# A planner's port rule, the RMS powers and the last norm's sums changed in a four-layer graph network kernel

## The chip, the core and the metric

The kernel runs on one core of a Trainium2 chip. The metric is the device time of one execution in microseconds (us), here the median of several. TensorE (PE) multiplies matrices, VectorE (DVE) and ScalarE (ACT) work on elements, GpSimd (POOL) takes powers, SyncE (SP) issues the transfers (DMA).

## What is computed

There are 32 independent graphs. Each has 512 nodes with 256 features (`x`) and a 512x512 weighted adjacency matrix (`adj`), and goes through four layers, all in fp32. Cut to what matters:

```python
# layer 0
x = layernorm(x + relu(((1 + eps) * x + adj @ x) @ W1 + b1) @ W2 + b2)       # 256 -> 512 -> 256
# layer 1
h = adj @ (x @ W.T + b);  x = layernorm(x + where(h > 0, h, alpha * h))
# layer 2
h = layernorm(x) * gamma + beta
x = layernorm(x + (x + relu((adj @ h) @ W_rel + b_rel + h @ W_root)))
# layer 3
h = (epsilon * x + adj @ x) @ W1 + b1                                        # 256 -> 1024
h = silu(h * rsqrt(mean(h * h, -1) + 1e-6) * rms_weight)                     # RMS norm, one factor per node
x = layernorm(x + h @ W2 + b2)
```

`layernorm` subtracts the mean over a node's features and divides by the square root of the variance plus 1e-5.

## The kernel before

**Blocks and products.** A graph's nodes lie as 128 partitions x 4 chunks (`NC = 4`). Each product (`aggregate`, `dense_feat`, `dense_add`) is cut into 2x2 blocks and made of seven block products instead of eight (`seven`, line 642): m1 to m7 are multiplied by TensorE into three PSUM banks, and between them VectorE or ScalarE reads a bank out (`take`, `put`). A bank is used by two or three products one after the other: the later product accumulates on the earlier one's result, so that it has to wait until the earlier one's `take` has read the bank. The block sums that the method needs (`left_sums`, `right_sums`, lines 660 and 668) are additions of VectorE. A graph has 106 matmuls with 256 columns and 112 with 128; the profile has two records for each.

**Order of the work.** The kernel first records every operation of all 32 graphs (`Plan.add`, line 247) with what it reads and writes, and with an estimated duration: the engine's busy time, and a tail until its result can be used (`vector_time`, `scalar_time`, `power_time` and so on, lines 32 to 63). `Plan.order` (line 350) then runs through time on these estimates. At each step it takes the engine that can start something first, and the operation of the lowest rank there. The rank is the graph's number times `period` plus the due time of the operation (`needs`, line 320). Up to five graphs are under way at once (`FLIGHT`), sharing 36 SBUF rooms and 8 banks. `best` (line 344) tries the entries of `RULES` (line 92) and takes the one whose plan ends first. The program then issues the operations in this order, each engine in its own queue; on the chip semaphores alone decide when one starts. An operation that ScalarE or VectorE can do goes to the one that the plan chose. As every operation is issued from the same line, the profile puts nearly all under L294.

**The port in the plan.** VectorE instructions with two operands in SBUF (`TWO_OPERANDS`, line 79) and GpSimd's are marked `port` (line 284). In the plan, a marked VectorE instruction holds GpSimd off until its end, and a GpSimd instruction holds marked VectorE work off for `PORT` = 0.25 us from the power's own start (lines 426 to 429).

**Norms.** Every inverse square root is a power of -0.5 by GpSimd (`inv_sqrt`, line 567): one of 128 partitions x 4 elements in each of layers 0, 2 and 3 (last norm), one of 128x8 in layer 1 (two scalings), one of 128x4 for the RMS norm. `Norm` (line 887) has ScalarE sum each chunk twice (`total`: an Identity with a sum, then a Square with the mean as bias), `NormOnVector` (line 938) has VectorE do it with bn_stats and bn_aggr. Layer 3's last norm uses `NormOnVector`, the others `Norm`.

**The RMS factor.** In layer 3 the squares of the 1024 features are added up by VectorE (`acc`). `column_sums` (line 866) reduces them with a transposing reduction and three additions to 32 partitions x 16. `everywhere` (line 975) then turns this into one factor per node along a row of all partitions: `by_token` (line 882) spreads the sums over 128 partitions x 4 in four small instructions, the power is taken, four more (`square`) bring it back to 32x16, a 32x32 transpose follows, and two transfers through DRAM (`line`) copy it to all partitions. The first and the last graph (`alone`) use TensorE for this instead.

**Transfers.** All go through SP's queue. `move` (line 304) has a `late` figure, extra time that the plan assumes: 1.0 for the loads of `x` and `adj`, 0.0 for `carry` (line 564), which moves blocks of transposed features within SBUF.

Of the kernel before, what the change touches and what calls it, by code (L numbers as in the profile page):

```python
# [20 lines left out]
def span(ap):  # L21

    n = 1
    for d in ap.shape[1:]:
        n *= d
    return n
# [33 lines left out]


def power_time(n):
    return 0.3 + n * 0.21, 0.04

# [10 lines left out]


TWO_OPERANDS = ("tensor_add", "tensor_sub", "tensor_mul", "scalar_tensor_tensor")
PORT = 0.25  # L80


SOON = 0.03
# [5 lines left out]

RULES = [(40, 2, 12, 0.25), (40, 2, 20, 0.25), (45, 2.5, 20, 0.25)]


class Pool:
# [104 lines left out]
class Op:  # L200
# [10 lines left out]
    behind: int = 0  # L211
    then: list = field(default_factory=list)
    start: float = 0.0
    way: str = ""


class Plan:
# [132 lines left out]
    def order(self, period, pace, last, near):  # L350

        final = max(op.graph for op in self.ops) - self.flight + 1
        rank = [
            (min(op.graph, final) * period + max(op.graph - final, 0) * last + need, i)
            for i, (op, need) in enumerate(zip(self.ops, self.needs(pace, near)))
        ]
        behind = [op.behind for op in self.ops]
        ready = [dict.fromkeys(op.ways, 0.0) for op in self.ops]
        left = {}
        for op in self.ops:  # L360
            left[op.graph] = left.get(op.graph, 0) + 1
            for r in op.rooms:
                r.clear()
                r.pool.clear()
        free = dict.fromkeys(("tensor", "vector", "scalar", "gpsimd", "sync"), 0.0)
        oldest, wire, lanes = 0, 0.0, [0.0] * LANES
        port = dict.fromkeys(free, 0.0)
        can_start = {i for i, n in enumerate(behind) if not n}
        done = []
        while can_start:  # L370
            while oldest in left and not left[oldest]:
                oldest += 1
            room_at = {}

            def rooms_free(op):

                first = [r for r in op.rooms if r.index is None]
                if not first:
                    return 0.0
                if op.graph - oldest >= self.flight:  # L380
                    return None
                at, taken = 0.0, {}
                for r in first:
                    pool = r.pool
                    if pool not in room_at:
                        room_at[pool] = pool.free()
                    whole, halves = room_at[pool]
                    k = taken.get((pool, False), 0)
                    if not r.whole and k < len(halves):
                        taken[pool, False] = k + 1  # L390
                        at = max(at, halves[k][0])
                        continue
                    n = taken.get((pool, True), 0)
                    taken[pool, True] = n + 1
                    n += pool.spare[min(op.graph - oldest, len(pool.spare) - 1)]
                    if n >= len(whole):
                        return None
                    at = max(at, whole[n][0])
                return at

            best = {}
            for i in can_start:
                op = self.ops[i]
                wait = rooms_free(op)
                if wait is None:
                    continue
                if op.kbytes and "sync" in op.ways:
                    wait = max(wait, lanes[0])
                at = {
                    e: max(free[e], wait, ready[i][e], port[e] if op.port else 0.0) for e in op.ways  # L410
                }
                way = min(
                    at, key=lambda e: at[e] + sum(op.ways[e][0]) + YIELD * (op.yields and e == "vector")
                )
                best.setdefault(way, []).append((at[way], rank[i], i))
            if not best:
                return 1e12, None
            t, engine = min((min(c)[0], e) for e, c in best.items())
            soon = t + (1e-6 if engine == "tensor" else SOON)
            _, t, i = min((r, s, i) for s, r, i in best[engine] if s <= soon)  # L420
            op = self.ops[i]
            op.start, op.way = t, engine
            busy, tail = op.ways[engine][0]
            free[engine] = t + busy
            end = t + busy + tail
            if op.port and engine == "vector":
                port["gpsimd"] = end
            elif op.port and engine == "gpsimd":
                port["vector"] = t + PORT
            if op.kbytes:  # L430
                wire = max(wire, t + ADVANCE) + wire_time(op.kbytes)
                end = wire + op.late + AFTER
                if engine == "sync":
                    lanes = [*lanes[1:], end]
            for r in op.rooms:
                if r.index is None:
                    r.pool.take(r)
                r.left -= 1
                r.until = max(r.until, end + 0.1)
            left[op.graph] -= 1  # L440
            for n, result in op.then:
                behind[n] -= 1
                for e in ready[n]:
                    if e != engine or e != "tensor" and result:
                        ready[n][e] = max(ready[n][e], end + HAND[e])
                if not behind[n]:
                    can_start.add(n)
            can_start.remove(i)
            done.append(op)
        return max(op.start for op in done), done  # L450
# [3 lines left out]
def tile_gnn_stack(ctx: ExitStack, tc: tile.TileContext, a: dict, out: bass.AP):  # L454
# [107 lines left out]
        plan.do(o, way)  # L562

    def carry(o, x):
        plan.move(o, x, o.shape[0] * span(o) / 256)

    def inv_sqrt(o, x):
        n, p = span(o), o.shape[0]
# [11 lines left out]
    def small(*shape):  # L580
        return Part(Room(smalls)).shaped(*shape)
# [25 lines left out]
    def constant(name, shape):  # L607
        return const.tile(shape, F32, tag=name, name=name)
# [22 lines left out]
    ctx.enter_context(nc.allow_non_contiguous_dma(reason="small vectors, once"))  # L631
    ident = constant("ident", [P, P])
    make_identity(nc, ident)
    mhalf = constant("mhalf", [P, 2 * NC])
    scraps = [constant(f"scrap{i}", [P, D]) for i in range(2)]
    nc.vector.memset(scraps[0], 0.0)
    nc.vector.memset(mhalf, -0.5)
    for tile_of_few in smalls.tiles:
        nc.vector.memset(tile_of_few, 0.0)

# [52 lines left out]
    class Adjacency:  # L693
# [3 lines left out]
        def __init__(self, b):  # L697

            self.halves = [room(HC, N) for _ in range(2)]
            for m in range(NC):  # L700
                chunk = self.halves[m // HC][:, m % HC, :]
                plan.move(chunk, a["adj"][b][:, m, :], P * N / 256, late=1.0)
            a11, a12, a21, a22 = (
                self.halves[j][:, :, i * TH : (i + 1) * TH] for i in range(2) for j in range(2)
            )
            self.left = dict(m1=a11, m2=a12, m4=a22)
            self.a21 = a21
# [174 lines left out]
    def by_token(o, sums, *ops):  # L882

        for q in range(P // Q):
            ts(o[q * Q : (q + 1) * Q], sums[:, q :: P // Q], *ops)
# [88 lines left out]

    def everywhere(sums, ops):

        few = small(2, NC)
        ve, power = few[:, 0, :], few[:, 1, :]
        by_token(ve, sums, *ops)
        inv_sqrt(power, ve)  # L980
        if alone():
            o = bank(N)
            for c in range(NC):
                flip(o[:, c * P : (c + 1) * P], power[:, c : c + 1].spread(P, P))
        else:
            few = small(2, Q)
            square, turned = few[0:Q, 0, :], few[0:Q, 1, :]
            for q in range(P // Q):
                ts(square[:, q : N // Q : P // Q], power[q * Q : (q + 1) * Q], 1.0, None, ALU.mult)
            plan.do(turned, vector("transpose", Q, square))  # L990
            o, line = short(N), next(lines)
            name = line.tensor.name
            plan.move(line.rearrange("(m i) -> m i", i=Q), turned[0 : N // Q], N / 256, into=name)
            plan.move(o, line.partition_broadcast(P), P * N / 256, late=0.8, outof=[name])
        return o
# [17 lines left out]

    def load_x(b):
        x = tok()
        plan.move(x, a["x"][b].rearrange("(p c) d -> p c d", c=NC), N * D / 256, late=1.0)
        return x

    def layer0(x, adjacency):
# [53 lines left out]
    def layer3(x, adjacency, b):  # L1073
# [17 lines left out]
        for q in range(0, FH, 2):  # L1091
# [2 lines left out]
                act(hT.chunk(f), hT.chunk(f), AF.Silu, scale=w_3[:, f : f + 1])  # L1094
            for m, t in dense_sums([hT.pair(q)], [hT.pair(FH + q)]).items():
                right[m] = right.get(m, []) + t
        norm = NormOnVector(x)
        dense_add(x, right, A2_3, norm.half)
        norm.scales((1.0, LN_EPS))
        y = norm.scaled()  # L1100
# [56 lines left out]

    with tc.manual_schedule():
        for op in plan.best():
            op.ways[op.way][1]()  # L1160


# [35 lines left out]
```

## Time and profile before

| | us |
|---|---|
| median of 3 runs | 2349.52 (2348.96 to 2350.26) |
| the profiled execution | 2349.14 |
| its span in the profile | 2347.2 |
| PE busy, DVE busy | 2305.1, 2209.5 |
| ACT busy, POOL busy | 1516.7, 233.3 |
| granted TensorE clock | 0.999 |
| VectorE waiting for TensorE, in all | 70.0 (52 times) |
| 128x4 powers, 128x8 powers, mean of one | 1.151 (128 of them), 2.671 (32) |

The profile comes from one execution. A row of a timeline says when an instruction (or several of one kind) started, how long it took, its engine, its source line, what it wrote and read (`room` is SBUF, `ps` is PSUM, `few` a small SBUF tile), its shape and, in brackets, how long the engine had idled before it and who released it. A row with "x3" runs from the first one's start to the last one's end; the end of one lies a little after the start of the next, so the cost of one in a queue is read from start to start. The chain of work that ended last is followed back from the last instruction, at each step to what released it. Busy time of PE is modelled at its ends, so a PE that is called busy can still hide short waits.

### The profile page before, as it was taken

What the parts mean: (1) busy time and instruction counts of PE and PEld (TensorE: products, weight loads), DVE (VectorE), ACT (ScalarE), POOL (GpSimd) and SP (SyncE); (2) the same over time, 40 slices, a digit from 0 to 9 for tenths busy, and PEclk for the clock granted to TensorE, in tenths of its full rate; (3) what the DMA queues carried; (4) which work ended last, traced back from release to release, by engine and by line L of the source; (5) the groups of instructions that cost most, each with busy time, mean ns of one, the idle gap of its engine ahead of it and who ended that gap; (6) DMA issues with size and microseconds to landing.
All of it is one profiled execution on the core that took longest, in us unless ns stands there. A gap on an engine that the chain in (4) does not pass through costs nothing.

```text
span 2347.2 us, 40710 instructions
## 1 busy us (share of the span) xinstructions
PE 2305.1 (98%) x14002; PEld 2095.8 (89%) x14002; DVE 2209.5 (94%) x5850; ACT 1516.7 (65%) x3918; POOL 233.3 (10%) x166
## 2 busy tenths in 40 slices
PE   9999999999999999999999999999999999999998
PEld 7888998999999999989999999999999989888897
DVE  8998999999999999999999999999999999998988
ACT  4675667666676665676666766657666567566764
POOL 0100011101011101011011111010110101011001
PEclk9999999999999999999999999999999999999999
DMA  7001222122221122211222211222112221121001
GB/s 238 21 17 19 64 55 52 30 59 61 56 58 27 56 59 64 54 37 43 60 62 54 59 25 57 61 57 57 35 48 59 63 57 48 37 59 50 19 10 45
DMA packets 223454, 122.79 MB, mean 52 GB/s; under 512 B 142864, under 2 KB 194320, under 8 KB 223248
## 3 DMA queue, kind: packets, MB, share of 16 engines
q1 hardware_dynamic: 223248, 120.20, 19.2%
q8 instruction: 110, 1.80, 0.3%
q14 instruction: 96, 0.79, 0.1%
HBM read 78.92 MB, written 24.97 MB: 44 GB/s over the span
## 4 chain that ended last, share of the span: by engine, by line
PE 84%; DVE 12%; DMA 1%; issue 1%; ACT 1%; SPq 0%; POOLq 0%; DVEq 0%; ACTq 0%
PE ps L294 84%; DVE room L294 10%; DVE few L294 2%; ACT room L294 1%; ACT scrap L294 0%; DMA diagonal<-room 0%; SPq L312 0%; DMA L_gnn_eps<-in_L_gnn_eps_dram 0%; DMA room<-in_x_dram 0%; DMA room<-room 0%; DMA room<-in_adj_dram 0%; DVE A L294 0%; POOLq L1194 0%; DVE L_gnn_W L294 0%; DVEq L294 0%
## 5 line engine op out<-in xcount | busy, mean ns | idle before, releaser
L294 PE MATMUL ps<-room,room 128*128 128x256 f32 x3584 | 931.7, 380 | 6.1 <-ACT room L294 2.6
L294 DVE TENSOR_TENSOR room<-room,room 128x512 f32<-128x512 f32 (+1 forms) x1360 | 778.0, 591 | 4.1 <-DMA room<-in_adj_dram 1.7
L294 PEld LDWEIGHTS ps<-room,room 128*128 128x128 f32 x3584 | 613.2, 191 | 62.7 <-ACT room L294 6.5
L294 DVE TENSOR_TENSOR room<-ps,room 128x256 f32<-128x256 f32 (+1 forms) x1344 | 599.1, 471 | 66.9 <-PE ps L294 65.6
L294 PE MATMUL ps<-L_gnn_W,room 128*128 128x128 f32 (+1 forms) x3584 | 583.2, 291 | 4.4 <-DVE room L294 2.2
L294 PEld LDWEIGHTS ps<-L_gnn_W,room 128*128 128x128 f32 x3584 | 539.0, 191 | 50.0 <-DVE room L294 5.0
L294 PEld LDWEIGHTS ps<-A,room 128*128 128x128 f32 x3072 | 466.3, 191 | 68.0 <-issue 17.1
L294 PE MATMUL ps<-A,room 128*128 128x128 f32 x3072 | 492.0, 276 | 17.3 <-DVE few L294 13.4
L294 POOL TENSOR_TENSOR few<-few,mhalf 128x4 f32<-128x4 f32 (+1 forms) x160 | 232.6, 1455 | 2108.2 <-DVE few L294 2084.2
L294 PE MATMUL ps<-room,L_gnn_W 128*128 128x256 f32 x1536 | 419.3, 380 | 3.1 <-DVE room L294 3.1
L294 ACT ACTIVATE room<-room,few 128x256 f32<-128x256 f32 x580 | 316.4, 597 | 121.7 <-DVE few L294 121.6
L294 ACT ACTIVATE room<-ps 128x256 f32<-128x256 f32 x514 | 187.9, 376 | 248.4 <-PE ps L294 247.1
L294 DVE TENSOR_TENSOR room<-room 128x256 f32<-128x256 f32 (+1 forms) x640 | 314.3, 496 | 34.4 <-DMA room<-room 13.4
L294 ACT ACTIVATE room<-ps,L_gnn_b_c 128x256 f32<-128x256 f32 x768 | 310.6, 478 | 50.7 <-PE ps L294 50.3
L294 PE MATMUL ps<-room,A 128*128 128x256 f32 x1152 | 323.4, 380 | 0.4 <-DVE room L294 0.2
L294 ACT ACTIVATE room<-room 128x1024 f32<-128x1024 f32 (+2 forms) x260 | 242.1, 945 | 122.4 <-DVE room L294 119.0
L294 PEld LDWEIGHTS ps<-room,L_gnn_W 128*128 128x128 f32 x1536 | 271.2, 191 | 32.2 <-DVE room L294 6.4
L294 ACT ACTIVATE scrap<-room 128x256 f32<-128x256 f32 x384 | 157.4, 411 | 172.3 <-DVE room L294 168.5
L294 ACT ACTIVATE scrap<-room,few 128x256 f32<-128x256 f32 x384 | 191.5, 499 | 77.6 <-DVE few L294 74.9
L294 PEld LDWEIGHTS ps<-room,A 128*128 128x128 f32 x1152 | 204.0, 191 | 21.5 <-ACT room L294 0.7
L294 ACT ACTIVATE room<-room,L_gnn_rms_weight_c 128x512 f32<-128x512 f32 x256 | 170.6, 711 | 28.0 <-DVE room L294 27.9
L294 DVE TENSOR_SCALAR few<-few 32x4 f32<-32x4 f32 (+2 forms) x792 | 119.0, 158 | 6.5 <-ACT scrap L294 0.6
(56 smaller groups left out, 1153.8 us busy)
## 6 DMA issues: line engine op xcount, KB each, us to landing
room<-in_adj_dram SPq DMA_DIRECT2D x128, 256.0 KB, 5.0
room<-in_x_dram SPq DMA_DIRECT2D x32, 512.0 KB, 6.0
out_dram<-room SPq DMA_DIRECT2D x32, 512.0 KB, 3.2
room<-room SPq DMA_DIRECT2D x480, 32.0 KB, 2.0
diagonal<-room SPq DMA_DIRECT2D x62, 128.0 KB, 1.8
room<-in_adj_dram SPq DMA_DIRECT2D x124, 64.0 KB, 1.9
room<-diagonal SPq DMA_DIRECT2D x62, 128.0 KB, 2.3
room<-line SPq DMA_DIRECT2D x30, 256.0 KB, 3.3
```

What stands on the lines that cost most here:

```text
L294: getattr(getattr(self.nc, engine), method)(to, *(put(x) for x in args), **kw)
```

## The change

It has five parts. `power_time`, `PORT` and `RULES` get other numbers, and the plan's port rule is another: after a VectorE instruction whose result a power uses, marked VectorE work is held off for 0.35 us from that instruction's end, and no longer by the power's start. Where the plan leaves VectorE idle for that reason, the program issues small memsets of a tile of its own (`pause`). The RMS power is taken directly on the 32 partitions x 16 of the sums, so that `by_token` and `square` go, but for the first and the last graph. Layer 3's last norm is a `Norm`, again but for these two. And the transfers are planned with longer `late` figures. The diff, its core:

```diff
 def power_time(n):
-    return 0.3 + n * 0.21, 0.04
+    return 0.3 + n * 0.18, 0.2 + 0.06 * n
...
-PORT = 0.25
+PORT = 0.35
...
-RULES = [(40, 2, 12, 0.25), (40, 2, 20, 0.25), (45, 2.5, 20, 0.25)]
+RULES = [(42, 2, 20, 0.5), (42, 2, 12, 0.25)]
...
+        powers = {i for i, op in enumerate(self.ops) if op.port and "gpsimd" in op.ways}
...
-            free[engine] = t + busy
+            free_before, free[engine] = free[engine], t + busy
             end = t + busy + tail
-            if op.port and engine == "vector":
-                port["gpsimd"] = end
-            elif op.port and engine == "gpsimd":
-                port["vector"] = t + PORT
+            if engine == "vector":
+                idle = t - max(free_before, ready[i][engine])
+                op.pause = idle if op.port and t == port[engine] else 0.0
+                if op.port:
+                    port["gpsimd"] = end
+                if any(n in powers for n, _ in op.then):
+                    port["vector"] = t + busy + PORT
...
     def carry(o, x):
-        plan.move(o, x, o.shape[0] * span(o) / 256)
+        plan.move(o, x, o.shape[0] * span(o) / 256, late=1.2)
...
-    mhalf = constant("mhalf", [P, 2 * NC])
+    mhalf = constant("mhalf", [P, N // Q])
...
-                plan.move(chunk, a["adj"][b][:, m, :], P * N / 256, late=1.0)
+                plan.move(chunk, a["adj"][b][:, m, :], P * N / 256, late=1.6)
...
     def everywhere(sums, ops):
-        few = small(2, NC)
-        ve, power = few[:, 0, :], few[:, 1, :]
-        by_token(ve, sums, *ops)
-        inv_sqrt(power, ve)
         if alone():
+            few = small(2, NC)
+            ve, power = few[:, 0, :], few[:, 1, :]
+            by_token(ve, sums, *ops)
+            inv_sqrt(power, ve)
...
         else:
-            few = small(2, Q)
-            square, turned = few[0:Q, 0, :], few[0:Q, 1, :]
-            for q in range(P // Q):
-                ts(square[:, q : N // Q : P // Q], power[q * Q : (q + 1) * Q], 1.0, None, ALU.mult)
+            few, turned = small(2, Q), small(Q)[0:Q]
+            ve, square = few[0:Q, 0, 0 : N // Q], few[0:Q, 1, :]
+            ts(ve, sums, *ops)
+            inv_sqrt(square[:, 0 : N // Q], ve)
             plan.do(turned, vector("transpose", Q, square))
...
-        plan.move(x, a["x"][b].rearrange("(p c) d -> p c d", c=NC), N * D / 256, late=1.0)
+        plan.move(x, a["x"][b].rearrange("(p c) d -> p c d", c=NC), N * D / 256, late=1.6)
...
-        norm = NormOnVector(x)
+        norm = (NormOnVector if alone() else Norm)(x)
...
         for op in plan.best():
+            if op.pause and op.way == "vector":
+                for _ in range(round(op.pause / 0.11)):
+                    nc.vector.memset(pause, 0.0)
             op.ways[op.way][1]()
```

More of the change, by code (lines that the diff above doesn't have):

```diff
@@ L213 @@
     start: float = 0.0
+    pause: float = 0.0
     way: str = ""
@@ L637, in tile_gnn_stack @@
     nc.vector.memset(mhalf, -0.5)
+    pause = constant("pause", [P, 48])
     for tile_of_few in smalls.tiles:
```

## The prediction

> **What bounds the kernel now.** I read the page's first section, then the chain of work that ended last, then the timelines of single engines around the one place where that chain leaves TensorE.
>
> ```profile
> span 2347.2 us, 40710 instructions
> ...
> PE 2305.1 (98%) x14002; PEld 2095.8 (89%) x14002; DVE 2209.5 (94%) x5850; ACT 1516.7 (65%) x3918; POOL 233.3 (10%) x166
> ...
> PE 84%; DVE 12%; DMA 1%; issue 1%; ACT 1%; SPq 0%; POOLq 0%; DVEq 0%; ACTq 0%
> ```
>
> TensorE is busy 98% of the time, so at most the rest, and what hides inside "busy", can be won. The chain in order of time, over two graphs in the middle:
>
> ```profile
> 1148.40 70.31 PE ps L294 x428
> 1218.71 0.01 issue
> 1218.72 1.17 PE ps L294 x8
> 1219.89 0.42 DVE room L294
> 1220.31 0.09 DVE few L294
> 1220.40 0.06 issue
> 1220.46 70.31 PE ps L294 x428
> ```
>
> The same piece begins at 1148.40 and at 1220.46: a period of 72.06 us, one graph, and the whole-span list of long pieces repeats it from 214 to 1872, 23 times. In each, TensorE runs 70.31 us unbroken and then waits for one VectorE instruction. How much is that worth? In the timeline of PE, 26 matmul records of 256 columns start 0.216 us apart (5.78 us less one 0.38, by 25) and 8 of 128 columns 0.111 apart. A graph has 106 matmuls of 256 and 112 of 128 columns, each two records: 212 x 0.216 + 224 x 0.1113 = 70.7 us. So a period holds 72.06 - 70.7 = 1.35 us that are not matmul work, about 1.0 at this break and the rest in tenths. For all 14002 records the same sum is 2271 us; of the other 76 us, 31 are in the 23 periods, about 10 before the first and after the last matmul, and about 35 in the start-up (to 214) and the last graphs (from 1872). The break itself, PE first and then DVE:
>
> ```profile
> 1218.11 0.60 PE L294 MATMUL ps<-room,room 128*128 128x256 f32 x2
> 1218.72 1.16 PE L294 MATMUL ps<-A,room 128*128 128x128 f32 x8
> 1220.46 1.13 PE L294 MATMUL ps<-A,room 128*128 128x128 f32 x8 [0.58 <-DVE few L294]
> ```
>
> ```profile
> 1217.59 1.08 DVE L294 TENSOR_TENSOR room<-ps,room 128x256 f32<-128x256 f32 x3
> 1218.59 0.68 DVE L294 TENSOR_TENSOR room<-room,room 128x512 f32<-128x512 f32 x1
> 1219.18 0.68 DVE L294 TENSOR_SCALAR few<-few 32x4 f32<-32x4 f32 x4
> 1219.89 0.42 DVE L294 TENSOR_TENSOR room<-ps,room 128x256 f32<-128x256 f32 x1
> ```
>
> These are layer 2's dense products (weights A, from `A_2`). Two records of 256 from 1218.11 should end their issue at 1218.54, and the next start at 1218.72; eight of 128 should give way at 1219.61, and the next start at 1220.46: 0.18 + 0.85 lost. In the built order the product that waits (m3) accumulates in the bank of m5, and m5's take is the add at 1219.89. VectorE has not idled: that take stands behind a 512-wide add and the four `square` instructions of the RMS power. So TensorE's one steady wait is VectorE being late.
>
> **The change, part by part.**
>
> *RMS powers on 32 partitions.* Out go, in 30 graphs (not the first and last, which are alone), four `by_token` and four `square` instructions; in comes one of 32x16. The row above prices four at 0.70 us (1219.18 to 1219.89), the new one at 0.15 by the 32x16 adds: 2 x 0.70 - 0.15 = 1.25 us of VectorE per graph. All four squares stood directly ahead of the awaited take, and the four `by_token` (0.67 us, at 1214.19) five microseconds ahead of it, with VectorE hardly idle between. In the built order of the changed kernel layer 2's seven products stand as before (between m5 and m3 again a product of four, one 256-column matmul and another product of four), but between the takes of m1 and m5 there are now one 512-wide add (0.60), one 128x4 (0.07) and the 32x32 transpose (0.12), 0.79 us, where there were 1.30. So the take comes 0.51 us earlier by the order alone, and up to 1.03 (the whole break) if the 0.5 us of the `by_token` carries through: I take 0.75.
>
> The power itself grows from 4 to 16 elements a partition. Its rows:
>
> ```profile
> 1150.15 1.01 POOL L294 TENSOR_TENSOR few<-few,mhalf 128x4 f32<-128x4 f32 x1 [6.03 <-DVE few L294]
> ...
> 1175.95 3.02 POOL L294 TENSOR_TENSOR few<-few,mhalf 128x8 f32<-128x8 f32 x1 [12.76 <-DVE few L294]
> ```
>
> The 128x8 power takes 1.64 in some graphs (at 169.05) and 3.02 in the periods. From 1.01 and 1.64 each element costs 0.158: 16 of them about 2.9 us, an estimate; with the delay of the 128x8 (1.38 for 8) doubled, 5.7. In the new order the work on VectorE between the instruction that releases it and the transpose that reads it sums to 6.1 us. So either way nothing waits. If VectorE ran ahead of that, the price would be the difference, some 2 us once a graph on the row's way to layer 3, whose transfers (1.3 and 3.3 us) lie ahead of products that are not due.
>
> *Two-operand work kept off the start of powers.* The plan now lets a one-operand or PSUM instruction follow each release. Where VectorE did adds of two SBUF operands through the start, the 128x8 power took 3.02; where an add from PSUM followed it (169.05), 1.64. So the powers will be short: 1.4 us for the 8, some 0.3 for the 4s. But it is worth nothing on the path: the late power's reader stands at 1179.59, after its end at 1178.97, and in the list of waits VectorE waited for GpSimd 2.9 us in the whole run, TensorE 0.3. Nothing becomes late instead. The pauses are 22 memsets in the built program, none in its repeating part; at 0.11 us (the 128x64 memset) at most 2.4 us, and I take 0.5, since they stand in the start-up and the end, half of which is VectorE's.
>
> Here a rule speaks against the longer power. The Trainium skill, "SBUF — State Buffer", "Who interferes with whom", says that VectorE with two SBUF inputs and a GpSimd instruction that reads SBUF exclude each other, the later one blocked until the first is done. By it each power would stop VectorE to its end: 2.9 us more a graph, 60 us in 21 periods, and the change would lose. The row says otherwise: within the power from 1150.15 to 1151.16 a 512-wide add of two SBUF operands starts at 1150.73 and takes 0.66 us, its usual time (mean 678 ns over 912). Only GpSimd is delayed. I go by the row: 0.
>
> *Last norm's sums by ScalarE.* Out go four BATCH_NORM_STATS2 (0.31 from start to start) and four aggregates (0.09) per graph; in come on ScalarE four Identity sums (0.42 from start to start, at 1169.27) and four Square sums (0.50, at 1174.40). VectorE gets 1.6 us, ScalarE 3.7. One scaling also moves to ScalarE in the new order (0.33 off, 0.55 on). ScalarE goes from 1084/23 = 47.1 to 51.3 us of a 72 us period: room enough in sum; that a copy is held up is the slow rival below. The functions are ones already in use, so no table loads come.
>
> *Longer transfers planned* (`late`), and new ranks: no instruction is added, and SP's queue holds the same 32 issues a graph. In a period VectorE has one wait for such a transfer (0.64 us, at 1197.16), and right after it waits 1.77 us for TensorE (at 1199.63), which hides it: I count 0, bounds -2 to 4 for the edges, where loads do end waits.
>
> **The sum.** VectorE loses 1.25 + 1.6 + 0.33 = 3.2 us of 68.6 (1578/23) a graph: 65.4 of 72, so it is no longer within 5% of TensorE's 70.7. Periods: the built order repeats exactly for 21 graphs, 21 x 0.75 = 16 us. Start-up and end: nine graphs of the thirty lie there, 9 x 3.2 = 29 us of VectorE work; the chain there is about a third VectorE, and part of the gaps are loads, so of about 35 lost us I take 6. Bounds: 12 if it follows VectorE's share in full, and -4, since the repeating part begins one graph later in the new order and a start-up graph loses some 5 us (18 to 214) where a period loses 1.35. Together 16 + 6 - 0.5 = 21.5. The profiled execution took 2349.14 (span 2347.2 and 1.9 around it); its difference from the median 2349.52 is 0.4. 2349.1 - 21.5 = 2327.6; I say **2328**.
>
> **The rivals.**
> - *The wait only moves.* VectorE's spare time falls where nobody waits, and another take is 1 us late each period in the new order, as greedy orders do. For: with VectorE at 65 of 72 there are still stretches without a gap. Against: the same seven products have lost just what held them. It leaves the edges: 2349 - 6 = 2343 (2338 to 2349).
> - *All waits go.* With VectorE clear, TensorE runs at its pitch: 21 x 1.35 = 28, edges 12: 2309 (2305 to 2317). Against: a third of the 1.35 are tenths from many takes.
> - *ScalarE becomes late (slower).* In the new order four sums (2 x 0.42 + 2 x 0.50 = 1.84 us) stand right ahead of a ScalarE copy out of an aggregate's bank. Between a product there and the next into its bank lie at least 1.1 us of other matmuls; less the copy (0.36) and about 0.3 of hand-off, 0.45 is to spare. If all 1.84 falls on it, TensorE waits 1.4 a period: 21 x 1.4 = 29, less 21.5: 2357. It decides from 0.45 + 21.5/21 = 1.5 us of delay. Against: ScalarE idles 20 us in 72, and TensorE waited 5.5 us for it in the run before.
>
> **How the numbers follow.** A measurement here tells about 0.2% (4.7 us) from no change. Chances: main case 0.58 (own range 2318 to 2338), the wait moves 0.20, all go 0.14, ScalarE 0.08. Faster by over 0.2% (below 2344.8): 0.57 + 0.14 + 0.12 = 0.83; the same: 0.10; slower: 0.07. For 8 in 10 the range takes in the likelier part of each neighbour: 2309 to 2345.
>
> **What would show it.** Right: a period near 71.3 us in the chain with its break at layer 2's products gone or below 0.3; VectorE near 2110 busy, ScalarE near 1640; 128x8 powers at 1.64, the 32x16 near 2.9 and no VectorE wait for it. Wrong: a period still near 72 with another instruction as releaser; TensorE waiting for ScalarE's copies; VectorE adds longer than 0.7 us inside the long power; or start-up and end longer than 214 and 475 us by more than the periods win.

## The result, and the profile after

| us | before | after |
|---|---|---|
| median (5 runs each, same chip) | 2350.26 (2348.96 to 2350.80) | 2339.10 (2337.50 to 2340.12) |
| profiled execution, its span | 2349.14, 2347.2 | 2338.08, 2336.3 |
| PE time beyond 2271 us of matmul work: start-up, middle, end | 19.5, 29.5, 18.5 | 21.0, 18.6, 17.0 |
| mean period, graphs 4 to 26 | 72.06 | 71.55 |

The ratio is 0.9953 (0.9938 to 0.9967): 11 us won where 21.5 were forecast. The third row applies the prediction's sum (0.216 us for a record of 256 columns, 0.1113 for one of 128) to the start of every matmul record: how much later than at full pitch it comes. "Start-up" is until 250 us of matmul work are issued, "middle" from there to 1800, "end" the rest up to the last matmul. All the gain is in the middle (10.9); the start-up lost 1.5 and the end won 1.5.

The page after, its heads and the chain's shares:

```profile
span 2336.3 us, 41057 instructions
...
PE 2304.8 (99%) x14002; PEld 2105.4 (90%) x14002; DVE 2139.5 (92%) x5411; ACT 1630.1 (70%) x4409; POOL 261.9 (11%) x166
...
PE 73%; DVE 22%; issue 2%; ACT 2%; DMA 1%; POOL 0%; SPq 0%; DVEq 0%; POOLq 0%; ACTq 0%
```

VectorE has 70 us less work (2209.5 before), ScalarE 113 more, and yet VectorE's share of the chain rose from 12% to 22%. The chain in order of time shows where it lies:

```profile
1210.91 55.36 PE ps L295 x324
1266.29 0.42 DVE room L295
1266.75 0.04 issue
1266.79 0.83 DVE room L295 x2
1267.62 0.38 issue
1268.00 4.02 DVE room L295 x7
...
1281.33 1.01 DVE room L295 x3
1282.34 0.04 issue
1282.38 7.65 PE ps L295 x54
```

Before, TensorE held the chain for 70.3 us of each graph and left it for one take. Now it leaves it for 16 us of VectorE work without slack. What that costs TensorE is small, as its own timeline shows at the end of this stretch:

```profile
1281.47 0.83 PE L295 MATMUL ps<-L_gnn_W_root,room 128*128 128x128 f32 x6
1282.38 1.13 PE L295 MATMUL ps<-room,room 128*128 128x256 f32 x4
```

Six records of 0.111 from 1281.47 end their issue at 1282.14: 0.24 lost, where the break before cost 1.03. Most periods are 71.48; five of 22 are 71.75 to 71.83.

The powers, by form, count, busy time and mean ns:

```profile
L295 POOL TENSOR_TENSOR few<-few,mhalf 128x4 f32<-128x4 f32 x98 | 101.6, 1037 | 756.6 <-DVE few L295 691.8 <-DVE pause L1168 64.8
L295 POOL TENSOR_TENSOR few<-few,mhalf 32x16 f32<-32x16 f32 x30 | 87.5, 2915 | 928.2 <-DVE few L295 926.1 <-DVE pause L1168 2.1
L295 POOL TENSOR_TENSOR few<-few,mhalf 128x8 f32<-128x8 f32 x32 | 72.9, 2278 | 383.9 <-DVE few L295 351.5 <-ACT room L295 32.4
```

The 32x16 power takes 2.9 us as estimated. The 128x8 fell only from 2.67 to 2.28; 1.64 was forecast for all, and most of those in the repeating part take 2.58.

In the start-up stands a wait that before did not have. ScalarE meanwhile makes six sums of other norms (101.29 to 104.62) ahead of two reads of banks. Behind the wait four records of 256 columns are 0.43 us apart instead of 0.216, at a granted clock of 0.50 from 104.9 to 108.3 (timeline of PE):

```profile
99.00 1.03 PE L295 MATMUL ps<-room,room 128*128 128x256 f32 x4
105.13 2.08 PE L295 MATMUL ps<-room,A 128*128 128x256 f32 x4 [5.11 <-ACT room L295]
```

### The profile page after: what moved, and what is told of

It reads as the page before. It is cut to its first block, busy times and chain, and to the rows that moved or that the text cites. A ratio compares the mean times of both kernels' runs of the same rounds, so it can differ in the third digit from the quotient of the medians.

```text
span 2336.3 us, 41057 instructions
## 1 busy us (share of the span) xinstructions
PE 2304.8 (99%) x14002; PEld 2105.4 (90%) x14002; DVE 2139.5 (92%) x5411; ACT 1630.1 (70%) x4409; POOL 261.9 (11%) x166
## 3 DMA queue, kind: packets, MB, share of 16 engines
q1 hardware_dynamic: 223248, 120.20, 18.8%
## 4 chain that ended last, share of the span: by engine, by line
PE 73%; DVE 22%; issue 2%; ACT 2%; DMA 1%; POOL 0%; SPq 0%; DVEq 0%; POOLq 0%; ACTq 0%
PE ps L295 73%; DVE room L295 19%; DVE few L295 2%; ACT room L295 1%; ACT scrap L295 1%; DMA L_gnn_W<-in_L_gnn_W_dram 0%; DMA L_gnn_ln_beta_c<-in_L_gnn_ln_beta_dram 0%; POOL few L295 0%; DMA room<-in_adj_dram 0%; SPq L313 0%; DVE A L295 0%; DVEq L295 0%; POOLq L1203 0%; DVE L_gnn_W_root L295 0%; DVE pause L1168 0%
## 5 line engine op out<-in xcount | busy, mean ns | idle before, releaser
L295 PEld LDWEIGHTS ps<-room,room 128*128 128x128 f32 x3584 | 625.6, 191 | 73.7 <-DVE room L295 10.0
L295 PE MATMUL ps<-L_gnn_W,room 128*128 128x128 f32 (+1 forms) x3584 | 539.5, 291 | 6.5 <-ACT room L295 4.5
L295 PEld LDWEIGHTS ps<-L_gnn_W,room 128*128 128x128 f32 x3584 | 505.1, 192 | 39.2 <-ACT room L295 5.7
L295 POOL TENSOR_TENSOR few<-few,mhalf 128x4 f32<-128x4 f32 (+2 forms) x160 | 261.1, 1638 | 2068.7 <-DVE few L295 1969.4
L295 PEld LDWEIGHTS ps<-A,room 128*128 128x128 f32 x3072 | 453.5, 191 | 37.3 <-DVE room L295 3.7
L295 PE MATMUL ps<-A,room 128*128 128x128 f32 x3072 | 467.3, 275 | 1.6 <-DVE room L295 1.5
L295 ACT ACTIVATE room<-ps 128x256 f32<-128x256 f32 (+1 forms) x515 | 180.6, 377 | 232.5 <-PE ps L295 231.5
L295 ACT ACTIVATE scrap<-room 128x256 f32<-128x256 f32 x504 | 206.7, 411 | 93.9 <-DVE room L295 84.2
L295 ACT ACTIVATE scrap<-room,few 128x256 f32<-128x256 f32 x504 | 251.9, 502 | 27.4 <-DVE few L295 25.4
L295 ACT ACTIVATE room<-room,L_gnn_rms_weight_c 128x512 f32<-128x512 f32 x256 | 173.6, 714 | 14.5 <-DVE room L295 14.3
L295 DVE TENSOR_TENSOR room<-room,loop 128x256 f32<-128x256 f32 x256 | 103.4, 411 | 4.1 <-PE ps L295 2.3
```

Source lines behind the costliest of these rows:

```text
L295: getattr(getattr(self.nc, engine), method)(to, *(put(x) for x in args), **kw)
```

## The experiments

Each was timed in several rounds beside the kernel before on one chip; "ratio" is to it, with a 95% interval. In the expectations, theory Q is that the length of VectorE's queue ahead of layer 2's take of m5 sets the gain, P that the new plan does (one thing in it is a clear start for the powers), S that the last norm's sums on ScalarE cost what is missing. Two kinds are kept apart: runs with a **fixed order** (only what is issued at a planned place is changed) and runs that are **planned anew**, where the planner may move everything.

| kernel | order | median us | ratio | start-up, middle, end | period |
|---|---|---|---|---|---|
| fix_rms | before's | 2345.1 | 0.9975 (0.9965 to 0.9985) | 18.5, 26.9, 17.9 | 71.94 |
| fix_rms_pause | before's | 2326.6 | 0.9898 (0.9884 to 0.9911) | 20.5, 8.8, 17.7 | 71.12 |
| after_four | after's | 2360.0 | 1.0036 (1.0022 to 1.0050) | 22.8, 37.1, 18.8 | 72.41 |
| after_nosums | after's | 2333.5 | 0.9928 (0.9915 to 0.9940) | 21.9, 15.6, 15.4 | 71.39 |
| moved_norm | no_norm's | 2366.6 | 1.0057 (1.0044 to 1.0069) | 26.3, 44.7, 14.1 | 72.67 |
| only_rms | anew | 2335.4 | 0.9934 (0.9922 to 0.9947) | 17.3, 18.6, 17.2 | 71.55 |
| only_norm | anew | 2363.8 | 1.0053 (1.0041 to 1.0066) | 17.6, 38.3, 29.5 | 72.49 |
| only_plan | anew | 2359.9 | 1.0039 (1.0027 to 1.0052) | 21.6, 34.0, 22.1 | 72.26 |
| rms_norm | anew | 2355.4 | 1.0017 (1.0009 to 1.0025) | 18.1, 38.2, 16.3 | 72.50 |
| no_norm | anew | 2326.8 | 0.9896 (0.9881 to 0.9911) | 28.0, 9.1, 11.2 | 71.12 |
| edge_norm | anew | 2333.4 | 0.9923 (0.9911 to 0.9936) | 27.0, 14.2, 11.6 | 71.36 |
| nn_late | anew | 2354.4 | 1.0011 (1.0005 to 1.0018) | 16.3, 44.0, 13.6 | 72.75 |
| nn_rules | anew | 2356.5 | 1.0020 (1.0014 to 1.0027) | 26.9, 25.8, 21.2 | 71.90 |
| nn_early1 | anew | 2321.8 | 0.9879 (0.9865 to 0.9892) | 20.3, 8.5, 11.1 | 71.11 |
| nn_early3 | anew | 2318.8 | 0.9863 (0.9848 to 0.9878) | 18.1, 8.5, 11.1 | 71.11 |

The split by start-up, middle and end, and the period, are those of one profiled execution, the median is that of several. In six of these executions the granted clock was 0.50 early in the start-up, between 11 and 18 us, for 3.4 us (fix_rms_pause, after_four, moved_norm, edge_norm, nn_rules) or 6.8 us (no_norm). no_norm's had lost 10.3 us by then (at 20 us), before's 6.6, and it took 2329.74 where its kernel's other executions took 2326.19 to 2327.08. So some 3 of its 28.0 us, an estimate from these figures, belong to that execution and not to the order.

### The RMS part in the order of before

```diff
 # fix_rms: of the nine operations of the old RMS path only three are issued, in the old places
-by_token x4 (128x4); power 128x4; square x4
+one tensor_scalar 32x16; power 32x16; one copy 32x16
 # fix_rms_pause: as fix_rms, and behind the instruction that releases the power
+for _ in range(3):
+    nc.vector.memset(pause, 0.0)
```

> The kernel before with its own order kept, instruction by instruction; in 30 graphs three of the four by_token and three of the four square instructions are left out and the power is the 32x16 one (one copy of its result stays). Nothing is planned anew. Theory Q (VectorE's queue ahead of the take of m5 holds TensorE): the take comes about 1.0 us earlier, the break of 1.03 us a period falls below 0.3, so 23 periods win 13 to 23 us: 2327 to 2337 where the kernel before takes 2350. Rival P (the new plan won the time, and the instructions that went away were in nobody's way): within 3 us of the kernel before.

Measured 2345.1, a quarter of what Q wanted. The timelines of POOL, DVE and PE in one graph of fix_rms say why:

```profile
1067.96 5.35 POOL L1003 TENSOR_TENSOR few<-few,mhalf 32x16 f32<-32x16 f32 x1 [23.33 <-DVE few L998]
```

```profile
1067.73 0.15 DVE L998 TENSOR_SCALAR few<-few 32x16 f32<-32x16 f32 x1
1067.81 0.74 DVE L294 TENSOR_TENSOR room<-room,loop 128x256 f32<-128x256 f32 x2
...
1073.35 0.16 DVE L1008 TENSOR_SCALAR few<-few 32x16 f32<-32x16 f32 x1 [1.20 <-POOL few L1003]
1073.44 0.40 DVE L294 TENSOR_TENSOR room<-ps,room 128x256 f32<-128x256 f32 x1
```

```profile
1072.08 1.05 PE L294 MATMUL ps<-A,room 128*128 128x128 f32 x8
1073.98 1.13 PE L294 MATMUL ps<-A,room 128*128 128x128 f32 x8 [0.85 <-DVE few L294]
```

Two adds with both operands in SBUF follow the release at 1067.73 and run across the power's start. The power then takes 5.35 us, not 2.9; its reader on VectorE waits 1.20 us, the take of m5 stands behind the reader, and TensorE loses 1.0 us (from 1072.97, where eight records of 0.111 end their issue, to 1073.98), as before: the new wait sits where the old work was. In two graphs of the same run the power took 3.01 and 3.34 us, and just their periods were 70.96. So the next run keeps the start clear.

> As the fixed-order kernel with six small instructions left out, and three memsets (0.12 us each) right behind the instruction that releases the RMS power, so that no add of two SBUF operands runs at the power's start. In the run without them the power took 5.35 us instead of 2.9 and VectorE's copy of its result waited 1.2 us for it, just ahead of the take that TensorE needs. Theory Q with the power's delay in it: the power takes 2.9, nothing waits for it, and the periods are those of the two graphs of that run whose power was short (70.96 instead of 72.04): 2322 to 2330. Rival (the wait for the power was not what held the take): 2342 to 2347.

```profile
1060.98 2.89 POOL L1006 TENSOR_TENSOR few<-few,mhalf 32x16 f32<-32x16 f32 x1 [23.33 <-DVE pause L1003]
```

2326.6, as expected: three memsets of 0.12 us each, from start to start, shortened the power by 2.46 us and the run by 18.6. TensorE's waits for VectorE's `few` (19 of them, 16.1 us, between 300 and 1800 us in fix_rms) are gone. So Q holds, once the power's start is kept clear, as the new plan also does. Theory P alone does not: the plan without the RMS part is slower than before (only_plan, below).

### The queue ahead of the take, in the order of after

```diff
 # after_four: six memsets ahead of the 32x32 transpose
+for _ in range(6):
+    nc.vector.memset(pause, 0.0)
 transpose(turned, square)
```

> The changed kernel with its own order, and six memsets (0.12 us each in this kernel's trace, 0.7 in sum) issued ahead of the 32x32 transpose in 30 graphs, which stands between the takes of m1 and m5: the VectorE time of the four square instructions is put back at their place. Theory Q: the period goes from 71.48 back by 0.4 to 0.7, so 8 to 15 us longer than the changed kernel: 2347 to 2354. Rival P: the new order has slack there: 2339 to 2341.

2360.0, beyond Q's range. DVE in the changed kernel, then DVE and PE at the same place of after_four:

```profile
1285.92 0.17 DVE L295 TENSOR_SCALAR few<-few 128x4 f32<-128x4 f32 x1
1285.99 0.19 DVE L295 STREAM_TRANSPOSE few<-few 32x32 f32<-32x32 f32 x1
1286.12 0.37 DVE L295 TENSOR_TENSOR room<-ps,room 128x256 f32<-128x256 f32 x1
```

```profile
1298.89 0.17 DVE L295 TENSOR_SCALAR few<-few 128x4 f32<-128x4 f32 x1
1299.01 0.97 DVE L1001 MEMSET pause<- 128x48 f32 x6
1299.90 0.14 DVE L295 STREAM_TRANSPOSE few<-few 32x32 f32<-32x32 f32 x1
1299.98 0.37 DVE L295 TENSOR_TENSOR room<-ps,room 128x256 f32<-128x256 f32 x1
```

```profile
1298.77 1.05 PE L295 MATMUL ps<-A,room 128*128 128x128 f32 x8
1300.49 1.13 PE L295 MATMUL ps<-A,room 128*128 128x128 f32 x8 [0.67 <-DVE room L295]
```

From the 128x4 to the transpose it is now 1.01 us, where it was 0.07: the six memsets cost 0.94 us and not the 0.7 expected, and each period grew by 0.86. TensorE waits for the take at 1299.98, the one that it waited for in before, again about once a graph (22 waits, 14.5 us, between 300 and 1800; the changed kernel has one of 0.3). Of the two theories only Q lets that work matter. The new order has less than 0.1 us of slack ahead of this take, so Q's number was too small by what the memsets were underpriced.

### One part at a time

```diff
 # only_rms / only_norm / only_plan / rms_norm: the kernel before with
+the RMS path on 32 partitions          # only_rms, rms_norm
+(NormOnVector if alone() else Norm)(x) # only_norm, rms_norm
+power_time, PORT, RULES, pause, late   # only_plan
```

> The kernel before with the RMS powers on 32 partitions alone, planned anew with the old figures. Theory Q: periods near 71.4, start-up and end unchanged or a few us either way: 2334 to 2342. Rival P: 2347 to 2353.

> The kernel before with layer 3's last norm summed by ScalarE alone, planned anew with the old figures. Theory Q: the squares still stand before the take, so the period keeps at least half of its break, and the ScalarE queue makes waits of TensorE at the start-up and the end (5 to 8 us in the changed kernel): 2342 to 2355. Rival N (the gain comes from the relief of VectorE anywhere, 1.6 us a graph): 2332 to 2342.

> The kernel before with the changed plan alone: power times, port rule and pauses, RULES, late figures; RMS powers and last norm as before. Theory Q: short powers free nobody as long as the four small instructions stay before the take: 2345 to 2354. Rival P (the plan itself won the time): 2335 to 2342.

> The plan of before, with the RMS part and the last norm's part. If the last norm's part costs its 12 us whatever the plan, this comes out at the run with the RMS part alone (2335) plus 12: 2343 to 2352. If its cost is one of the changed plan alone, it stays at 2330 to 2338. If the two parts help each other without the plan, below 2330.

The RMS part alone, in its expected range, is faster than all parts together (2335.4); the norm's part alone and the plan's part alone are slower than before, both by more than expected, and rms_norm came out above its range. Compared at their medians, alone the three make -15.5, +12.8 and +9.0 us against before, in sum +6; together they make -11. Costs of parts that are planned anew do not add up.

### The last norm left as it was

```diff
 # no_norm (changed kernel)                 # edge_norm: NormOnVector in the first 4 and last 5 graphs
-norm = (NormOnVector if alone() else Norm)(x)
+norm = NormOnVector(x)
```

> The changed kernel without the change of layer 3's last norm (bn_stats by VectorE in all graphs), planned anew with the changed plan. Theory S (the sums on ScalarE cost more at the start-up and the end than VectorE's relief wins): 2322 to 2335, faster than the changed kernel's 2339. Rival N (the relief of VectorE is what makes the periods short): 2343 to 2352.

> The changed kernel, with the last norm by VectorE in the first four and the last five graphs and by ScalarE between them, planned anew. If the waits of TensorE for ScalarE in the start-up (5.1 us) and the last graphs (2.3 us), and the 3.4 us stretches of half clock after them (about 1.7 us each), come from layer 3's sums there, they go: 2326 to 2334. If they come from the other norms and the order, they stay: 2336 to 2343.

no_norm took 2326.8: without its last-norm part the change gains 24 us. That is in S's range, but not where S had it: of what the part costs, 9.5 us are in the middle (18.6 for 9.1) and 5.8 at the end (17.0 for 11.2), and the start-up of no_norm is the longer one. At the end TensorE's waits for ScalarE, from 1800 us on, are 4.8 us in the changed kernel and 0.4 in no_norm. The chain of no_norm in the middle is one piece:

```profile
1194.86 80.29 PE ps L295 x499
```

edge_norm's 2333.4 lies in the range for "the waits go" by the end alone (11.6 for 17.0): the start-up wait of 5.1 us for ScalarE is in both runs, so it does not come from layer 3's sums. Two fixed orders say how the norm's part costs:

```diff
 # moved_norm: no_norm's order; at the old places ScalarE's sums are issued
-bn_stats x4, bn_aggr x4 (VectorE)
+Identity sum x4, Square sum x4 (ScalarE)
 # after_nosums: after's order; the sums are planned but not issued
-total(first, ...); total(second, ...)
```

> The order of the run without the last norm's part is kept to the last instruction, and only in the 28 middle graphs the last norm's four BATCH_NORM_STATS2 and four aggregates give way to four Identity and four Square sums on ScalarE, put where the old ones were issued, with two small VectorE instructions. If it is the planned order that cost the 12 us (the planner, with ScalarE's sums in it, moves other things), this run stays at that of the kernel without the part or below, 2320 to 2330, since VectorE is freed of 1.6 us a graph. If it is ScalarE's queue itself (3.7 us a graph of sums ahead of copies that TensorE waits for, and the squares behind the identities' round over VectorE), it comes out at 2332 to 2350, with new waits of TensorE for ScalarE at the end of each graph.

In moved_norm the scale of the second half of the nodes is also read before its sums are made, since the old order puts that reader first; all instructions are issued. It took 2366.6, 40 us more than no_norm. ACT and PE there:

```profile
1119.69 0.51 ACT L984 ACTIVATE scrap<-room,few 128x256 f32<-128x256 f32 x1 [0.89 <-DVE few L979]
...
1121.18 0.49 ACT L984 ACTIVATE scrap<-room,few 128x256 f32<-128x256 f32 x1
...
1121.67 1.57 ACT L295 ACTIVATE room<-room,few 128x256 f32<-128x256 f32 x3
1123.15 0.81 ACT L295 ACTIVATE room<-ps,L_gnn_b_c 128x256 f32<-128x256 f32 x2
```

```profile
1121.75 0.61 PE L295 MATMUL ps<-A,room 128*128 128x128 f32 x4
1124.02 0.70 PE L295 MATMUL ps<-room,A 128*128 128x256 f32 x2 [1.66 <-ACT room L295]
```

Four Square sums, 1.98 us from 1119.69 to 1121.67, stand ahead of the read of a bank (1123.15) that TensorE waits for, and had themselves waited 0.89 us for VectorE. TensorE's wait comes once a graph (20 times, 33.2 us, between 300 and 1800); the period is 1.55 us longer, and the run longer than the queue theory expected. The planner, knowing of the sums, avoids this in the changed kernel (between 300 and 1800 us PE's list of waits holds a single one, 0.3 us for VectorE), at a price:

> The order of the changed kernel is kept to the last instruction; in the 28 middle graphs the last norm's eight sums are planned but not issued, so the norm works on old values and ScalarE is freed of 3.7 us a graph. If the sums themselves cost the 12 us by standing in ScalarE's queue, the time falls to 2325 to 2331, with the period at 71.1. If the price lies in the order that the planner makes around them (the queue as such being clear of TensorE), it stays at 2336 to 2340 with the period at 71.5.

2333.5, as neither theory had it: 5.6 us below the changed kernel, 6.8 above no_norm. Of the profiled spans' 3.7 us, 3.0 is in the middle (0.16 a period), 1.6 at the end, and the start-up takes 0.9 back. So the issue of the sums is about half of the part's 12 us, and the order made around them the other half. By the intervals of the ratios each half is uncertain by some 4.5 us.

### The planned landing of transfers

```diff
 # nn_late: no_norm with the old late figures     # nn_early3, nn_early1: only in the first 3, 1 graphs
-late=1.2 / 1.6 / 1.6
+late=0.0 / 1.0 / 1.0
 # nn_rules: no_norm with the old rules
-RULES = [(42, 2, 20, 0.5), (42, 2, 12, 0.25)]
+RULES = [(40, 2, 12, 0.25), (40, 2, 20, 0.25), (45, 2.5, 20, 0.25)]
```

> The kernel without the last norm's part, with the old figures for the landing of transfers (0, 1.0, 1.0 for 1.2, 1.6, 1.6). If these figures bring the start-up wait of TensorE for ScalarE of 5.1 us (and the 3.4 us at half clock behind it), the wait goes and the time is 2317 to 2324. If the ranking rules bring it, the wait stays and the time is 2325 to 2332, and the figures for landing are worth nothing. If the old figures were too short for the transfers, waits of VectorE for the DMA come back in the start-up and the time is over 2330.

> The kernel without the last norm's part, with the old three ranking rules. If the new rules bring the start-up wait of 5.1 us for ScalarE, it goes and the time is 2317 to 2324 with the period at 71.1. If not, it stays and the time is 2325 to 2332. If the old rules also give another repeating order, the period tells it: above 71.3 would be worse than 2330.

nn_late is 28 us slower than no_norm, but its start-up is 11.7 us shorter and without the 5.1 us wait. In the middle VectorE now meets transfers that have not landed (DVE, then PE):

```profile
1356.71 1.29 DVE L295 TENSOR_TENSOR room<-room,room 128x512 f32<-128x512 f32 x2 [1.23 <-DMA room<-in_adj_dram]
1357.92 0.42 DVE L295 TENSOR_TENSOR room<-ps,room 128x256 f32<-128x256 f32 x1
```

```profile
1358.40 1.16 PE L295 MATMUL ps<-A,room 128*128 128x128 f32 x8 [0.81 <-DVE room L295]
```

The plan with the old figure lets an adjacency load land 4.0 us after its issue (1.5 + 1.0 + 256/385 + 0.8), with the new one 4.6; the pages of before and after show a median of 5.0 and 5.1. But such waits come to 9.0 us in 11 times between 300 and 1800, and waits of VectorE for powers to 11.8 us in 13 times; no_norm has neither there. They are a part of the 35 us by which that stretch grew; the rest is not explained beyond another order. nn_rules lost in the middle; the 5.1 us wait near 105 us is gone there too, and another of 4.4 us for ScalarE stands at 165. So the wait near 105 us takes the new figures together with the new rules, and the new figures are needed later. Can they be undone for the first graphs alone?

> The kernel without the last norm's part, with the old figures for the landing of transfers in the first three graphs alone. If those figures bring the start-up wait of 5.1 us for ScalarE (it was gone with the old figures throughout), the start-up gets 8 to 13 us shorter while the period stays at 71.1: 2314 to 2320. If the new figures only happened to give another order, any order may come out: 2325 to 2345, with the wait there or not.

> As the run with the first three graphs, with the old figures for the landing of transfers in the first graph alone. If the wait stems from the first graph's transfers, 2314 to 2320; if from those of the next two, 2325 to 2329 with the wait still there; if orders fall out by chance, anything from 2315 to 2345.

2318.8, as expected, and 2321.8, between the two ranges: the start-up falls from 28.0, some 3 of which belong to that one execution, to 18.1 and 20.3 (in the second, waits of 1.9 and 2.3 us for ScalarE are left), and the middle and the end stay within 0.6 us of no_norm's. nn_early3 is the best of the study, 0.9863 (0.9848 to 0.9878) of before: the changed kernel without its last-norm part, and with the old landing figures for its first three graphs.

## Why the mechanism was right and the sum was not

- **Bound and mechanism: right; the range: luck.** 2339.1 lies in the stated 2309 to 2345 only because that takes in half of "the wait only moves" (2338 to 2349); the main case's own range ended at 2338. And that rival fits by its number alone: it has no gain in the periods and 6 us at the edges, and the runs show 10.9 and 0. The take of m5 behind the small RMS instructions was the steady wait. In before's own order taking them away made the period 0.94 us shorter (72.06 to 71.12), inside the forecast 0.51 to 1.03, of which 0.75 was taken.
- **"Periods: the built order repeats exactly for 21 graphs, 21 x 0.75 = 16 us": mis-sized for this kernel, 10.9.** The changed kernel's order gives 0.51 a period on the mean (0.58 in most), without the sums 0.67; no_norm's order gives 0.94.
- **"Last norm's sums by ScalarE", priced at nothing on the path: the step that failed.** "Room enough in sum" (51.3 us of 72) says nothing on what stands ahead of what. The part costs 12.3 us (2339.1 against 2326.8), more than the 10.3 by which the forecast gain was too large. The slow rival had the mechanism: "1.4 a period" from four sums ahead of a copy, 1.55 in moved_norm. That the sizes are so close is partly luck, since there it is four Squares and a wait of their own. The rival was treated as all or nothing; that the planner could dodge the wait and pay with a worse order was not among the cases.
- **"Start-up and end: 6": failed, 0.0.** The bounds were -4 to 12, and the reason given for the lower one is not what counted. The longer landing figures, priced at 0 with a bound of 4, bring the start-up wait of 5.1 us together with the new rules: undoing them for three graphs is worth 8.0 us in no_norm (2326.8 to 2318.8). The wait is in the changed kernel too; that undoing them gains as much there is not shown. At the end the sums hold up TensorE, and the granted clock is 0.50 for 3.4 us twice (from 2036.8 and 2313.3; in before it is 1.00 at both places).
- **"Worth nothing on the path" for the powers' starts: wrong in before's order, harmless here.** The estimate of 2.9 us uncontended (2.89 in 28 of 30 graphs of the changed kernel) and the bound of 5.7 contended (5.35) were good. The cover of 6.1 us held only in the changed order; in before's it was 4.3 (from 1067.81 to 1072.15, where the wait of 1.20 begins), and the shortfall cost 18.6 us a run.
- **The rule and the row: right about VectorE, and half a picture.** The Trainium skill, "SBUF — State Buffer", "Who interferes with whom", has the two exclude each other, the later one blocked. In the rows looked at VectorE is not stopped: the two adds from 1067.81, over the start of the 5.35 us power, go at 0.33 us from start to start, as the add from PSUM ahead of them does (1067.40 to 1067.73). GpSimd is held up, as the rule says, where the adds are there first, though not every time (see the last section). The row shown, of a power that began before the add, could not tell that.
- **128x8 at 1.64: only some.** Mean 2.28. Nothing waited for it in the repeating part.
- **DVE and ACT busy** were forecast near 2110 and 1640: 2139.5 and 1630.1.

Open: why the order with the sums in it is the worse one outside the sums' own time (6.8 us), and by which wait the sums cost the 0.16 us a period; no wait of TensorE in the middle names ScalarE.

## What to carry to other kernels

When an order is planned by a greedy scheduler, price an edit twice: in the fixed order, where its own waits show, and planned anew, where anything may move (here a spread of 45 us among plans of nearly equal work). Sums moved to an engine with free time cost what stands behind them in that engine's queue, and what the plan gives up to keep that clear, not its busy share. A longer instruction on a slow engine needs its cover counted from its contended duration, and a few cheap instructions behind its release can buy that contention off.

## What was not expected of the hardware

A power is delayed by what VectorE does at its start, and not by the same work later. With adds of two SBUF operands across its start the 32x16 power took 5.35 us, with three memsets ahead of them 2.89, though such adds run inside both. The long one ends at 1073.31 as if it had begun at 1070.42; VectorE's run of such adds, from 1067.81 with one 128x2 instruction between, gives way to an add from PSUM at 1070.49. Before, an add that began 0.58 us into a power delayed it by nothing (1.01 us, as others).

But adds across the start are not enough. In the two short graphs of fix_rms the same instructions stand there in the same order (POOL and DVE):

```profile
1356.16 3.01 POOL L1003 TENSOR_TENSOR few<-few,mhalf 32x16 f32<-32x16 f32 x1 [23.33 <-DVE few L998]
```

```profile
1355.92 0.15 DVE L998 TENSOR_SCALAR few<-few 32x16 f32<-32x16 f32 x1
1356.00 0.81 DVE L294 TENSOR_TENSOR room<-room,loop 128x256 f32<-128x256 f32 x2
```

The two adds take 0.81 us here and 0.74 in the graph with the 5.35 us power; in the other short graph (3.34 us) it is the 128x2 instruction behind them that takes 0.17 for 0.15. So the places differ by hundredths of a us. Whether these let the power in or come of its being in, no run here shows.

The half clock came after short waits, and not each time. In the changed kernel two waits of 0.98 and 1.30 us for ScalarE, at 2033.8 and 2035.9, were followed by 3.4 us at a granted clock of 0.50; in after_nosums waits of 0.97 and 1.30 at the same place were not. The same piece of both, first the changed kernel:

```profile
2038.11 1.91 PE L295 MATMUL ps<-room,room 128*128 128x256 f32 x4
```

```profile
2034.54 1.03 PE L295 MATMUL ps<-room,room 128*128 128x256 f32 x4
```

The difference at this place is about 1.7 us (5.33 lost against 3.64 in the 72 us around it). The Trainium skill, "TensorE: Matmul & The Clock Gate", "Part 1: The HAM clock gate", has the half rate after an idle window of about 3.4 us, until a busy one of about 3.4 us. The 3.4 us from 2036.8 agree with the second, and the half clock behind the start-up's 5.1 us wait with the first; but at 2036.8 waits of 2.28 us in two pieces were enough. By the page's idle window this place would have stayed at full clock and cost 1.7 us less.
